# Where the split activations lie in SBUF: x2's high and low parts moved to multiples of 512 bytes

## The chip, the cores and the metric

The kernel runs on one core of one Trainium2 chip. The metric is the device time in microseconds (us), as a median over runs. Inside a core, TensorE (PE) multiplies matrices, VectorE (DVE) and ScalarE (ACT) work on 128-partition tiles, GpSimd (POOL) sums over partitions and issues some transfers, SyncE (SP) issues transfers. SBUF is the memory that the engines read; each tile is a piece of every partition, beginning at a byte address that is the same in all 128 partitions.

## The reference

One block of an RWKV-like network on x of shape (2, 4096, 256), hidden width 1024:

```python
x = x + attn(layernorm(x))     # time mixing, k, v, r, a scan over time, output product
x = x + ffn(layernorm(x))

def ffn(x):                    # x: 256 features
    h = silu(x @ w1.T * w1_s) * (x @ w2.T * w2_s)     # 256 -> 1024, twice
    h = gelu(h @ h1.T * h1_s)                         # 1024 -> 1024
    h = gelu(h @ h2.T * h2_s)                         # 1024 -> 1024
    return h @ w3.T * w3_s                            # 1024 -> 256
```

In attn, k, v, r and the output are products of 256 x 256 weights; the scan carries a log-max and a numerator along 4096 steps.

## The kernel before

Features lie on partitions, time along the free axis. The work is cut into 16 tiles of 512 steps (2 batches x 8). Each tile runs attention and then the FFN. The main loop runs the FFN of tile i and, step by step between its sums, attention of tile i + 1 and the first layernorm of tile i + 2, so that PE always has products to do.

The FFN's weights are ternary, so one fp32r pass holds them exactly. The activations are not, so each activation is split into a high part (rounded to fp32r) and a low part (the rest), and split_product issues two fp32r matmuls for every block of 128 features: L186 with the high part as the moving operand, L187 with the low part, both 128x512, both summed into the same PSUM tile. Attention's products (L179) are plain float32 and show as two matmuls each in the trace.

In the FFN of one tile:

- pa and pb (w1 and w2): 8 columns x 2 sums x 2 blocks x 2 parts = 64 matmuls, moving operands x2_hi and x2_lo. Each of these holds two blocks of 512 float words (2048 bytes) per partition.
- ph (h1, then h2): 2 x 8 columns x 8 blocks x 2 parts = 256 matmuls, moving operands hi and lo, 16 buffers of 2048 bytes each.
- po (w3): 2 x 8 x 2 = 32 matmuls, moving operands hi and lo.

ACT rounds the high parts (L193, L612), DVE takes the low parts (L194, L615). x2 itself is the output of the second layernorm, and x2_hi and x2_lo are made of it by split (L191).

Addresses come from the pools, which are laid one behind another in the order in which they are made: flags, const, x, wide, one, tmp, hid, stream. Within a pool each tag has its buffers, of the size of its largest tile, rounded up to 32 bytes. A tile in an early pool that grows or shrinks therefore moves everything behind it.

The names that the change touches: mean_wr (L136), a 128x128 fp32r tile that holds 1/256, with which the first tile's means are summed on PE (mean_w is the same tile read as float32) and which keep_warm (L372) multiplies with itself to keep PE busy in the first 39 us (results unread); num (L247), the numerator's states; each (L400), in the first tile's layernorm; and any_inexact (L636), which in the last tile's FFN sums a count over the partitions with one small product (everywhere, L641), to decide whether a general form of the block must run afterwards (it does not for these inputs).

Of the kernel before, what the change touches and what calls it, by code (L numbers as in the profile page):

```python
# [9 lines left out]
F32 = mybir.dt.float32  # L10
F32R = mybir.dt.float32r
# [3 lines left out]
P = 128  # L15
B, T, D, HID = 2, 4096, 256, 1024
TS = 512
# [49 lines left out]
def split_block(ctx, tc, flags, x, vecs, w_attn, w1, w2, h1, h2, w3, out):  # L67
# [3 lines left out]
    tensor, vector, scalar = nc.tensor, nc.vector, nc.scalar  # L71

    const = ctx.enter_context(tc.tile_pool(name="const", bufs=1))
    xpool = ctx.enter_context(tc.tile_pool(name="x", bufs=3))
    wide = ctx.enter_context(tc.tile_pool(name="wide", bufs=4))
    one = ctx.enter_context(tc.tile_pool(name="one", bufs=1))
    tmp = ctx.enter_context(tc.tile_pool(name="tmp", bufs=3))
    hid = ctx.enter_context(tc.tile_pool(name="hid", bufs=16))
# [54 lines left out]

    each_mean = hid.tile([P, P], F32, tag="hi", name="each_mean")
    vector.memset(each_mean, 1.0 / D)
    mean_wr = const.tile([P, P], F32R, name="mean_wr")  # L136
    vector.tensor_copy(mean_wr, each_mean)
    mean_w = mean_wr.bitcast(F32)
    vector.memset(eps, LN_EPS)
# [32 lines left out]
    def col(base, j):  # L172
        return vec[:, base + j : base + j + 1]
# [64 lines left out]
    def wkv(h, k, v, r, y, first):  # L238

        w, u = col(DECAY, h), col(FIRST, h)  # L240

        def pair(tag):
            both = one.tile([P, 2, TS], F32, tag=tag, name=tag)
            return [both[:, k, :] for k in range(2)]


        lm, num = (one.tile([P, TS + 1], F32, tag=tag, name=tag) for tag in ("lm", "num"))  # L247
        if first:
            vector.memset(lm[:, 0:1], LOG_ZERO)
            vector.memset(num[:, 0:1], 0.0)  # L250
        else:
            vector.tensor_copy(lm[:, 0:1], log_max[:, h : h + 1])
            vector.tensor_copy(num[:, 0:1], numer[:, h : h + 1])

        sc = pair("sc")


        so = pair("so")  # L260
        with tc.issue_after(marks["y"].ins) if h else nullcontext():
            vector.tensor_tensor_scan(lm[:, 1:], w.to_broadcast([P, TS]), k, lm[:, 0:1], ALU.add, ALU.max)  # L262
        vector.scalar_tensor_tensor(sc[1], lm[:, 0:TS], w, k, ALU.add, ALU.subtract)
        vector.tensor_scalar(sc[0], sc[1], NEG_CLAMP, 0.0, ALU.max, ALU.min)
        vector.tensor_scalar(sc[1], sc[1], 0.0, -NEG_CLAMP, ALU.max, ALU.min)
        scalar.activation(sc[0], sc[0], AF.Exp)
        scalar.activation(sc[1], sc[1], AF.Exp, scale=-1.0)
        vector.scalar_tensor_tensor(so[1], k, u, lm[:, 0:TS], ALU.add, ALU.subtract)
        vector.tensor_scalar(so[1], so[1], NEG_CLAMP, -NEG_CLAMP, ALU.max, ALU.min)
        vector.tensor_copy(log_max[:, h : h + 1], lm[:, TS:])  # L270
        scalar.activation(so[0], so[1], AF.Sigmoid, scale=-1.0)
        scalar.activation(so[1], so[1], AF.Sigmoid)
        scalar.activation(r, r, AF.Sigmoid)
        yield
        vector.tensor_tensor(sc[1], sc[1], v, ALU.mult)
        vector.tensor_tensor_scan(num[:, 1:], sc[0], sc[1], num[:, 0:1], ALU.mult, ALU.add)
        vector.tensor_copy(numer[:, h : h + 1], num[:, TS:])
        yield
        vector.tensor_tensor(so[0], so[0], num[:, 0:TS], ALU.mult)
        vector.tensor_tensor(so[1], so[1], v, ALU.mult)  # L280
        vector.tensor_tensor(so[0], so[0], so[1], ALU.add)
        marks["y"] = vector.tensor_tensor(y[:, h, :], so[0], r, ALU.mult)
        yield
# [23 lines left out]
    def attention(i):  # L307
# [18 lines left out]
        for h in range(ND):  # L326
            kvr = []
            for m, name in enumerate("kvr"):
                ps = ps_attn.tile([P, TS], F32, tag="pa", name="ps_" + name)
                product(  # L330
                    ps, lambda c: wa_sb[:, m, c, h * P : (h + 1) * P], [mixed[m][:, c, :] for c in range(ND)]
                )
                kvr.append(ps)
            yield
            yield from wkv(h, *kvr, y, first)
# [20 lines left out]
    def on(engine, operation, *args, **kwargs):  # L356
        with behind(engine):
            last[engine] = getattr(getattr(nc, engine), operation)(*args, **kwargs)  # L358

    def matmul(*args, **kwargs):  # L360
        on("tensor", "matmul", *args, **kwargs)

    def activation(*args, **kwargs):
        on("scalar", "activation", *args, **kwargs)

    def add(out, a, b, op=ALU.add):
        on("vector", "tensor_tensor", out, a, b, op)
# [12 lines left out]
    def first_layernorm(src, xc, means):  # L380

        sq = wide.tile([P, ND, TS], F32, tag="wide", name="sq")
        for mean, p in zip(means, halves):
            for h in range(ND):
                add(xc[:, h, p], src[:, h, p], mean, ALU.subtract)
            activation(sq[:, :, p], xc[:, :, p], AF.Square)
        varis = []
        for p in halves:  # L390
            add(sq[:, 0, p], sq[:, 0, p], sq[:, 1, p])
            var = ps_ffn.tile([P, TS // 2 // P], F32, tag="pf", name="var")
            for b in range(TS // 2 // P):
                t = slice(p.start + b * P, p.start + (b + 1) * P)
                matmul(var[:, b : b + 1], sq[:, 0, t], mean_w[:, 0:1], start=True, stop=True)
            varis.append(var)
            yield
        spread = []
        for var in varis:
            each = tmp.tile([P, TS // 2 // P], F32, tag="each", name="each")  # L400
            activation(each, var, AF.Sqrt, bias=eps)
            on("vector", "reciprocal", each, each)
            rstd = ps_ffn.tile([P, TS // 2], F32, tag="pf", name="rstd")
            for b in range(TS // 2 // P):
                matmul(
                    rstd[:, b * P : (b + 1) * P], each[:, b : b + 1].to_broadcast([P, P]), ident, start=True, stop=True
                )
            spread.append(rstd)
            yield
        for rstd, p in zip(spread, halves):  # L410
            for h in range(ND):
                add(xc[:, h, p], xc[:, h, p], rstd, ALU.mult)
            yield

    def first_tile(second):
# [3 lines left out]
        lm, num, sc, so = ([] for _ in range(4))  # L419
        for h in range(ND):  # L420
            pool, tags = ((one, ("lm", "num")), (stream, ("h2", "h2")))[h]
            for states, tag, start in zip((lm, num), tags, (LOG_ZERO, 0.0)):
                states.append(pool.tile([P, TS + 1], F32, tag=tag, name="state"))
                vector.memset(states[h][:, 0:1], start)
            for scales, tag in ((sc, "sc"), (so, "so")):
                if h:
                    scales.append([hid.tile([P, TS], F32, tag=t, name="scale") for t in ("hi", "lo")])
                else:
                    both = one.tile([P, 2, TS], F32, tag=tag, name="scale")
                    scales.append([both[:, k, :] for k in range(2)])  # L430
# [5 lines left out]
        for p in halves:  # L436
# [3 lines left out]
            means.append(mean)  # L440
        keep_warm(unread, 11, 2 * P)
        norm = first_layernorm(x_sb, xn, means)


# [120 lines left out]
        x2_hi = one.tile([P, ND, TS], F32R, tag="x2_hi", name="x2_hi")  # L565
        x2_lo = one.tile([P, ND, TS], F32R, tag="x2_lo", name="x2_lo")
        norm = first_layernorm(x_sb, x2, means)
        for _ in range(4):
            next(norm)
# [66 lines left out]
    def any_inexact():  # L636

        total = flags.tile([P, 1], F32, name="total")
        vector.tensor_reduce(total, rounded, mybir.AxisListType.X, ALU.add)
        everywhere = ps_attn.tile([P, 1], F32, tag="pa", name="everywhere")  # L640
        tensor.matmul(everywhere, mean_w, total, start=True, stop=True)  # L641
        inexact = flags.tile([P, 1], mybir.dt.int32, name="inexact")
        vector.tensor_scalar(inexact, everywhere, 0.0, None, ALU.is_gt)
        return inexact
# [4 lines left out]
    normal, got = {}, {}  # L649
    second = normalise(1)  # L650
    first_tile(second)
    with behind("gpsimd"):
        load_rest()
# [307 lines left out]
```

## Time and profile before

| what | value |
|---|---|
| median of 3 runs | 1541.54 us (1541.45 to 1542.15) |
| the profiled execution | 1540.95 us |
| its span, first to last instruction | 1539.4 us |
| mean granted TensorE clock | 0.999 |
| PE busy | 1529.8 us, 6260 matmuls |
| DVE, ACT, POOL busy | 69%, 68%, 16% of the span |
| starts of the FFN of tiles 0, 1, 2, 15 | 39.2, 134.0, 228.2, 1452.0 us |
| distance of two such starts, tiles 1 to 10 | 94.15 us |
| last matmul | 1532.2 us |

A row of the profile names the line, the engine, the operation, and written tile <- read tiles; then the count, busy time and mean duration, and the idle time of the engine before it. Matmuls overlap: the next begins before the one before it has ended. The rate at which PE works is therefore the distance between starts, which the timeline shows, and not the duration.

### The profile page before, as it was taken

To read this page: it belongs to the slowest core of one execution; us is meant where nothing else is said; L and a number is where in the kernel's file an instruction comes from. 1 tells how busy PE (TensorE), PEld (TensorE's weight loads), DVE (VectorE), ACT (ScalarE), POOL (GpSimd) and SP (SyncE) were. 2 spreads that over 40 slices of the span, in tenths; PEclk is the share of its full clock that TensorE was granted. 3 is DMA by queue.
4 is the path that set the end of the run, shared out by engine and by line. 5 is a ranking of instruction groups with operands and counts; after the bars stand their busy time and mean duration, and the time that the engine had idled before them with its cause. 6 is when DMAs were issued, how large, how long until landed. Compare 5 with 4: busy or idle time off the path is not lost.

```text
span 1539.4 us, 16523 instructions
## 1 busy us (share of the span) xinstructions
PE 1529.8 (99%) x6260; PEld 1172.8 (76%) x6260; DVE 1069.8 (69%) x1598; ACT 1047.3 (68%) x1348; POOL 240.5 (16%) x118
## 2 busy tenths in 40 slices
PE   9999999999999999999999999999999999999998
PEld 6778787777877778777787777877777787777886
DVE  7886676866768677785777768677686777855531
ACT  6685957759587595866858668595775858656542
POOL 4131021110211101112011121101111021100100
PEclk9999999999999999999999999999999999999999
DMA  7612030220302103031130311203122030210302
GB/s 274 137 55 89 14 118 33 82 69 14 134 18 96 55 26 133 7 110 42 45 113 14 117 35 59 93 10 120 35 77 74 14 130 21 96 41 28 117 9 83
DMA packets 39702, 109.16 MB, mean 71 GB/s; under 512 B 3712, under 2 KB 12672, under 8 KB 39104
## 3 DMA queue, kind: packets, MB, share of 16 engines
q1 hardware_dynamic: 25760, 79.86, 15.8%
q0 software_dynamic: 13296, 27.53, 5.7%
q8 instruction: 51, 0.84, 0.2%
q10 hardware_dynamic: 560, 0.66, 0.1%
q14 instruction: 35, 0.29, 0.1%
HBM read 99.64 MB, written 12.58 MB: 73 GB/s over the span
## 4 chain that ended last, share of the span: by engine, by line
PE 98%; DVE 1%; ACT 1%; issue 0%; DVEq 0%; ACTq 0%
PE ph L186 30%; PE ph L187 30%; PE pa L186 4%; PE pb L186 4%; PE po L187 4%; PE po L186 4%; PE pa L187 4%; PE pb L187 4%; PE ps_k L179 3%; PE ps_o L179 3%; PE ps_r L179 3%; PE ps_v L179 3%; PE ps_k L358 0%; PE unread L358 0%; DVE scale L358 0%; PE ps_v L358 0%
## 5 line engine op out<-in xcount | busy, mean ns | idle before, releaser
L186 PE MATMUL ph<-hi,h_sb 128*128 128x512 f32 x2048 | 815.7, 399 | 0.2 <-ACT hi L193 0.2
L187 PE MATMUL ph<-lo,h_sb 128*128 128x512 f32 x2048 | 811.5, 397 | 0.0
L186 PEld LDWEIGHTS ph<-hi,h_sb 128*128 128x128 f32 x2048 | 384.6, 188 | 98.5 <-issue 18.2
L187 PEld LDWEIGHTS ph<-lo,h_sb 128*128 128x128 f32 x2048 | 384.5, 188 | 96.9 <-issue 15.3
L207 POOL PARTITION_ALL_REDUCE total<-both x60 | 205.1, 3419 | 857.6 <-DVE both L205 442.7
L615 DVE TENSOR_TENSOR lo<-full,hi 128x512 fp32r<-128x512 f32 x256 | 197.2, 773 | 140.0 <-ACT full L614 137.1
L612 ACT ACTIVATE hi<-ph,vec 128x512 fp32r<-128x512 f32 x256 | 175.6, 686 | 125.7 <-PE ph L187 124.6
L596 ACT ACTIVATE gated<-pa,vec 128x512 f32<-128x512 f32 x128 | 87.4, 683 | 139.0 <-PE pa L187 137.2
L614 ACT ACTIVATE full<-ph,vec 128x512 f32<-128x512 f32 x256 | 175.3, 685 | 0.3
L597 DVE SCALAR_TENSOR_TENSOR gated<-pb,vec,gated 128x512 f32<-128x512 f32 x128 | 95.9, 749 | 70.9 <-PE pb L187 66.6
L612 ACT ACT_TABLE_LOAD x103 | 132.1, 1283 | 1.8
L231 DVE RECIPROCAL rstd<-rstd 128x256 f32<-128x256 f32 x60 | 102.8, 1731 | 2.1 <-ACT rstd L227 2.1
L193 ACT ACTIVATE hi<-gated 128x512 fp32r<-128x512 f32 x128 | 80.4, 628 | 33.8 <-DVE gated L597 33.5
L186 PE MATMUL pa<-x_hi,w_sb 128*128 128x512 f32 x256 | 101.9, 398 | 0.1
L186 PE MATMUL pb<-x_hi,w_sb 128*128 128x512 f32 x256 | 101.8, 398 | 0.0
L187 PE MATMUL pb<-x_lo,w_sb 128*128 128x512 f32 x256 | 100.5, 392 | 0.0
L187 PE MATMUL pa<-x_lo,w_sb 128*128 128x512 f32 x256 | 100.4, 392 | 0.0
L194 DVE TENSOR_TENSOR lo<-gated,hi 128x512 fp32r<-128x512 f32 x128 | 96.3, 760 | 4.8
L187 PE MATMUL po<-lo,w_sb 128*128 128x512 f32 x256 | 99.6, 389 | 0.0
L186 PE MATMUL po<-hi,w_sb 128*128 128x512 f32 x256 | 99.6, 389 | 0.0
L621 DVE SCALAR_TENSOR_TENSOR x_sb<-po,vec,x_sb 128x512 f32<-128x512 f32 x32 | 24.0, 751 | 72.1 <-PE po L187 72.1
L262 DVE TENSOR_TENSOR_SCAN lm<-vec,lm,ps_k 128x512 f32<-128x512 f32 x30 | 38.4, 1279 | 40.7 <-PE ps_k L179 40.7
(145 smaller groups left out, 1741.3 us busy)
## 6 DMA issues: line engine op xcount, KB each, us to landing
h_sb<-h_hbm SPq DMA_DIRECT2D x128, 512.0 KB, 3.2
raw<-in_h SPq DMA_DIRECT2D x32, 256.0 KB, 2.7
x_sb<-in_x POOLq DMA_DIRECT2D x15, 512.0 KB, 4.1
out<-x_sb POOLq DMA_DIRECT2D x15, 512.0 KB, 3.2
h_sb<-in_h POOLq DMA_DIRECT2D x1, 4096.0 KB, 18.7
h_hbm<-in_h POOLq DMA_DIRECT2D x8, 512.0 KB, 8.6
w_sb<-in_w POOLq DMA_DIRECT2D x3, 1024.0 KB, 9.6
raw<-in_w SPq DMA_DIRECT2D x12, 256.0 KB, 2.5
```

Of the source, the lines that this page charges most:

```text
L179: tensor.matmul(psum, weights(c), src[c], start=c == 0, stop=c == n - 1)
L186: tensor.matmul(psum, weights(c), hi, start=c == 0, stop=False)
L187: tensor.matmul(psum, weights(c), lo, start=False, stop=c == n - 1)
L193: marks["rounded"] = scalar.activation(hi, full, AF.Copy)
L194: marks["rest"] = vector.tensor_tensor(lo, full, hi.bitcast(F32), ALU.subtract)
L207: marks["sum"] = nc.gpsimd.partition_all_reduce(everywhere, both, channels=P, reduce_op=ReduceOp.add)
L231: vector.reciprocal(rstd[:, p], rstd[:, p])
L596: scalar.activation(full, pa, AF.Silu, scale=col(S1, f))
L597: vector.scalar_tensor_tensor(full, pb, col(S2, f), full, ALU.mult, ALU.mult)
L612: scalar.activation(hi, ps, AF.Gelu, scale=col(scales, f))
L614: marks["rounded"] = scalar.activation(full, ps, AF.Gelu, scale=col(scales, f))
L615: marks["rest"] = vector.tensor_tensor(lo, full, hi.bitcast(F32), ALU.subtract)
```

## The change

mean_wr takes a buffer of hid's tag "lo" in place of one of its own in const (512 bytes less there). num's buffer, in the pool "one" ahead of sc, so, both, total, x2_hi, x2_lo and xn, is made 32 words longer (2080 to 2208 bytes with rounding). each's three buffers, in tmp, grow from 32 to 160 bytes, so that what lies behind them (the tag "full", then hid and stream) stays where it was: -512 + 128 + 384 = 0. Since the buffer of mean_wr is given to activations later, the product at the end of the last tile reads a tile of ones, set just before, instead.

```diff
-    mean_wr = const.tile([P, P], F32R, name="mean_wr")
+    mean_wr = hid.tile([P, P], F32R, tag="lo", name="mean_wr")
...
-        lm, num = (one.tile([P, TS + 1], F32, tag=tag, name=tag) for tag in ("lm", "num"))
+        lm = one.tile([P, TS + 1], F32, tag="lm", name="lm")
+        num = one.tile([P, TS + 33], F32, tag="num", name="num")[:, : TS + 1]
...
-            each = tmp.tile([P, TS // 2 // P], F32, tag="each", name="each")
+            each = tmp.tile([P, 40], F32, tag="each", name="each")[:, : TS // 2 // P]
...
-                states.append(pool.tile([P, TS + 1], F32, tag=tag, name="state"))
+                states.append(pool.tile([P, TS + (33 if tag == "num" else 1)], F32, tag=tag, name="state")[:, : TS + 1])
...
-        tensor.matmul(everywhere, mean_w, total, start=True, stop=True)
+        ones = tmp.tile([P, P], F32, tag="full", name="ones")
+        vector.memset(ones, 1.0)
+        tensor.matmul(everywhere, ones, total, start=True, stop=True)
```

Where tiles begin in a partition, in bytes, and the remainder by 512:

| tile | before | after |
|---|---|---|
| w1_sb, w2_sb, h1_sb, w3_sb | 25088, 33280, 41472, 74240 (all 0) | the same |
| mean_wr | 82432 (0) | 181760 (0) |
| x_sb, first buffer | 83264 (320) | 82752 (320) |
| wide tiles, first buffer | 95552 (320) | 95040 (320) |
| sc, so | 116096, 120192 (384) | 115712, 119808 (0) |
| x2_hi, x2_lo | 128384, 132480 (384) | 128000, 132096 (0) |
| full, first buffer | 142848 (0) | the same |
| hi, lo, first buffers | 148992, 181760 (0) | the same |

The order of the instructions is the same on every engine, but for the memset of ones on DVE (behind the low part of column 5 in the last tile's second hidden layer) and the product everywhere, which stands five matmuls later on PE, inside column 7's sum, and waits for that memset.

## The prediction

> **What bounds the kernel now.** I read the first part of the page first (busy time per engine), then the chain that ended last, then the costliest groups.
>
> ```profile
> PE 1529.8 (99%) x6260; PEld 1172.8 (76%) x6260; DVE 1069.8 (69%) x1598; ACT 1047.3 (68%) x1348; POOL 240.5 (16%) x118
> ...
> PE 98%; DVE 1%; ACT 1%; issue 0%; DVEq 0%; ACTq 0%
> ...
> L186 PE MATMUL pb<-x_hi,w_sb 128*128 128x512 f32 x256 | 101.8, 398 | 0.0
> L187 PE MATMUL pb<-x_lo,w_sb 128*128 128x512 f32 x256 | 100.5, 392 | 0.0
> ...
> L187 PE MATMUL po<-lo,w_sb 128*128 128x512 f32 x256 | 99.6, 389 | 0.0
> L186 PE MATMUL po<-hi,w_sb 128*128 128x512 f32 x256 | 99.6, 389 | 0.0
> ```
>
> TensorE is never without work: the chain is 98% PE, and the view of waits gives PE 2.6 us of waiting in all, nearly all of it before 37 us. So the end is set by the beat at which one product follows another. The durations in the groups (389 to 398 ns) overlap and are not that beat; the starts in the timeline are. Two windows of PE's timeline, the same form of product (128x512, fp32r) on both sides; columns are start and duration in us:
>
> ```profile
> 418.81 0.40 PE L186 MATMUL pa<-x_hi,w_sb 128*128 128x512 f32 x1
> 419.04 0.39 PE L187 MATMUL pa<-x_lo,w_sb 128*128 128x512 f32 x1
> 419.27 0.40 PE L186 MATMUL pb<-x_hi,w_sb 128*128 128x512 f32 x1
> 419.51 0.39 PE L187 MATMUL pb<-x_lo,w_sb 128*128 128x512 f32 x1
> ...
> 420.91 0.39 PE L187 MATMUL pa<-x_lo,w_sb 128*128 128x512 f32 x1
> ```
>
> ```profile
> 503.83 0.39 PE L186 MATMUL po<-hi,w_sb 128*128 128x512 f32 x1
> 504.06 0.39 PE L187 MATMUL po<-lo,w_sb 128*128 128x512 f32 x1
> ...
> 505.65 0.39 PE L186 MATMUL po<-hi,w_sb 128*128 128x512 f32 x1
> 505.87 0.39 PE L187 MATMUL po<-lo,w_sb 128*128 128x512 f32 x1
> ```
>
> From 418.81 to 420.91 lie nine products that read x2's parts: 2.10 / 9 = 233.3 ns each. From 503.83 to 505.87 lie nine that read hi and lo: 2.04 / 9 = 226.7 ns. With the trace's nanoseconds it is sharper: in each of tiles 1 to 15 the 64 products of pa and pb take 14,925 ns from the first start to the start of ph, that is 233.2 ns, in pairs of 237.5 and 229.3; the 32 of po hold 226.65 to 226.68 in every tile. The granted clock is 1.00 in both stages.
>
> What differs is where the moving operand begins. Counting the pools' sizes, hi, lo, the weights and mean_wr all begin at a multiple of 512 bytes; x2_hi and x2_lo begin at 128384 and 132480, both 384 past one. They are the only moving operands of an fp32r product that do.
>
> **The change part by part.**
>
> *x2's place.* mean_wr leaves the constants (minus 512 bytes for all that follows), num grows from 2080 to 2208 bytes (plus 128), so x2_hi and x2_lo move by 384 down, to 128000 and 132096: remainder 0. The 64 products of a tile should then take the beat of po: 64 x 226.67 = 14,507 ns, 418 ns less. The first three products of ph still carry 15 ns of excess after x2 (beats 231, 233, 231); they go too. That is 433 ns for each of tiles 1 to 15. Tile 0 has 545 ns of excess, of which 107 are its first beat (334 ns, after the products that keep the clock up), which I leave: 438 ns. Sum: 15 x 0.433 + 0.438 = 6.93 us.
>
> Is a beat of 226.7 granted at once? After the two-pass f32 products (ps_r at 438.5 us) the next nine beats of ph, from 440.43 on, run to 232 on average and only then 226.7, about 0.05 us of settling. Ahead of pa lies po, already settled, so I expect none; with it, 16 x 0.05 = 0.8 us would come back. I take 0 and keep 0.8 for the range.
>
> *Does PE then wait for somebody?* The tightest place is the first sum of ph, whose last product reads lo of column 7. In the steady tiles that lo ends 2.84 us after ph's start, and the product that reads it starts at 3.42: 0.57 us of cover. DVE waits 0.32 us for pb ahead of column 7's gating (431.68 us), so it has no backlog and its work moves along with PE; even if all 0.433 us came off the cover, 0.14 would be left. x2 of the next tile is ready 8 to 13 us before its pa. Cost 0; if the cover were gone, at most the 0.43 us of a tile.
>
> *ones and the count.* One memset on DVE and no change on ACT, POOL and SP's order. The nearest row is each_mean's memset of the same size, 165 ns, once. It stands behind lo of column 5 in the last tile's second hidden layer, which ends at 1519.9 us. The product everywhere moves five products later, into column 7's sum, so about 1522.4 us; it now waits for the memset, done 2 us before. Behind it on DVE is queued lo of column 6, started at 1522.83 before; it may slip by some 0.3 us, and po needs it near 1527.9. The product itself cost PE about 0.25 us with its settling (beats 26, 112, 313, 236, 228, 233, 231 around 1521 us) and costs that again; 0 to 0.1 us either way. Cost 0.
>
> *mean_wr among the lo buffers.* It takes the first of 16; the two scales and the two scaled weights of the first tile take others. Its last reader is PE's last unread product (about 39 us), ahead of all FFN products on the same engine, so nobody waits for its buffer. It still begins at a multiple of 512. Cost 0.
>
> *The other tiles that move.* sc, so, both, total and xn go from remainder 384 to 0 (rstd of the second norm from 416 to 32), and only DVE, ACT and POOL touch them. The first tile shows that DVE does not mind: the same sum of shares takes 0.69 us at 24.40 us (h = 0, remainder 384) and 0.69 us at 28.82 us (h = 1, among hi and lo, remainder 0). About ten such instructions lie on the first tile's path; 10 ns each way makes 0.1 us. x_sb and the wide tiles keep their remainder (320). Cost 0, with 0.1 us to both sides.
>
> So 6.93 us come off. The profiled execution took 1540.95 us (span 1539.4); it should become 1534.0 (span 1532.5). The median of the runs is 1541.54, 0.59 above that execution, so the forecast is 1541.54 - 6.93 = 1534.6 us.
>
> *Rules that speak against it.* Other operands in the trace do not mind their place: the two-pass f32 products of ps_k, whose mx begins 320 past a multiple of 512, start every 429 ns (four from 435.05 to 436.76 us), and so do those of the first tile whose xn is shifted by 4 bytes. They stream at about half the rate, so a slow fetch may hide. [...]
>
> **The rivals.**
>
> 1. *Something other than the place sets the 233.3.* pa and pb alone change the bank after every 4 products (ph and po after 16), and read the same four moving blocks over and over. Then nothing changes: 1541.5 us. Against it: in tile 0 pa and pb alternate product by product at first, and the beat is the same 237 and 229; the slow half even falls on x_lo there and on x_hi later, so it goes with the order, not with the tile or the bank. The last tile, with no attention beside it, has the same beat, so it is no other engine. 7%. The same time would result if the place did not move; the sizes above leave no room for that.
>
> 2. *The new place is worse (slower).* All fast operands of the trace, hi, lo and mean_wr, begin at 512 past a multiple of 1024; x2's parts will begin at 0. If the fetch minds the place within 1024, x2 lands in a class that no row shows. Priced as the excess doubled: 1024 products x 6.6 ns = 6.8 us more, 1548.3 us. It decides from a beat over 236.3 ns (3.08 us / 1024 more). Against it: each operand is 2048 bytes long and passes both kinds of boundary anyhow. 4%.
>
> 3. *Better than the rest.* By the same unseen class the beat could fall below 226.7. A two-pass product's pass takes 429.2 ns; if half of that, 214.6, were one pass's floor, up to 1024 x 12.1 = 12.4 us more would go: 1522.2 us. No row supports it. 3%.
>
> 4. *Part of it comes back*, by settling at each start of pa or a lo that comes late: half of the gain, 1538.1 us. The cover of 0.57 us speaks against it. 4%.
>
> **How the numbers follow.** The forecast has 82%. Its own range is 1533.9 to 1536.2: the spread of the three runs (0.7 us) either way, and on the slow side the 0.8 of settling and 0.1 for moved tiles. I stretch the upper end to 1537.0, so as to take in a good part of rival 4, and the lower one to 1533.5 for the 0.1 us bounds and the profiled execution's 0.59 us. A measurement of this kernel tells about 0.2% (3.1 us) from no change, so faster means under 1538.5: 82 + 3 and most of rival 4, 88%. The same: 7% and a little of rival 4, 8%. Slower: 4%.
>
> **What would show it.** In the profile after, starts of pa and pb 226.7 ns apart, hi and lo alike; their group means at 389 as in po; 14.51 us instead of 14.93 from pa's first start to ph; starts of pa 93.72 us apart instead of 94.15; ph, po and the f32 products unchanged. A beat still at 237 and 229 makes rival 1 right; any other beat, rival 2 or 3; a new wait of ph for lo (L194), rival 4.

## The result, and the profile after

The changed kernel takes 1534.89 us (median of 6 runs, 1534.75 to 1535.13) against 1541.58 us before (6 runs): a ratio of 0.9957, 95% interval 0.9947 to 0.9967. The median fell by 6.69 us. The forecast was 1534.6 us (6.93 less), range 1533.5 to 1537.0.

The page of the changed kernel, the lines that answer to those shown of before (busy time per engine, the chain, the groups of pa and pb):

```profile
PE 1523.0 (99%) x6260; PEld 1172.8 (76%) x6260; DVE 1071.1 (70%) x1599; ACT 1047.5 (68%) x1348; POOL 241.9 (16%) x118
...
PE 98%; DVE 1%; ACT 1%; DMA 0%; issue 0%; DVEq 0%
...
L186 PE MATMUL pb<-x_hi,w_sb 128*128 128x512 f32 x256 | 99.6, 389 | 0.0
...
L187 PE MATMUL pb<-x_lo,w_sb 128*128 128x512 f32 x256 | 99.6, 389 | 0.0
```

PE's busy time is 6.8 us shorter with the same 6260 matmuls; DVE and ACT do the same work but for one memset. The means of pa and pb went from 398 and 392 to 389, what po had already. The starts say it directly (PE's timeline in tile 4; columns are start and duration in us):

```profile
419.04 0.39 PE L186 MATMUL pa<-x_hi,w_sb 128*128 128x512 f32 x1
419.27 0.39 PE L187 MATMUL pa<-x_lo,w_sb 128*128 128x512 f32 x1
419.49 0.39 PE L186 MATMUL pa<-x_hi,w_sb 128*128 128x512 f32 x1
...
421.08 0.39 PE L187 MATMUL pa<-x_lo,w_sb 128*128 128x512 f32 x1
```

Nine beats from 419.04 to 421.08: 2.04 / 9 = 226.7 ns, high and low alike. In tiles 1 to 15 the 64 products of pa and pb take 14,506 or 14,507 ns (14,925 before), the first three beats of ph have no excess left, and starts of pa are 93.72 us apart (94.15 before).

The span of the profiled execution fell by 6.1 us, not by 6.93 (that of before was 0.59 us under its median, as the prediction says). Tiles 1 to 15 gave what was forecast: 14 distances between starts, 6.07 us together, and 0.43 in tile 15. Three things of 0.1 to 0.3 us lie outside them. The first start of pa came at 39.47 us instead of 39.16; DVE waited 3.3 instead of 3.0 us for the first x. The kernels below, whose heads are alike but for small memsets, have it between 39.2 and 40.0, so that is no property of the change that these runs could show. Tile 0 gave back most of its part (below). The stretch from the start of the last matmul to the end was 0.12 us longer (7.18 and 7.30; the kernels below have 7.1 to 7.5).

### The profile page after: what moved, and what is told of

Its sections match the earlier page's. It is cut to its first block, busy times and chain, and to the rows that moved or that the text cites. A ratio compares the mean times of both kernels' runs of the same rounds, so it can differ in the third digit from the quotient of the medians.

```text
span 1533.3 us, 16524 instructions
## 1 busy us (share of the span) xinstructions
PE 1523.0 (99%) x6260; PEld 1172.8 (76%) x6260; DVE 1071.1 (70%) x1599; ACT 1047.5 (68%) x1348; POOL 241.9 (16%) x118
## 4 chain that ended last, share of the span: by engine, by line
PE 98%; DVE 1%; ACT 1%; DMA 0%; issue 0%; DVEq 0%
PE ph L186 30%; PE ph L187 30%; PE po L187 4%; PE po L186 4%; PE pa L186 4%; PE pa L187 4%; PE pb L186 4%; PE pb L187 4%; PE ps_k L179 3%; PE ps_o L179 3%; PE ps_v L179 3%; PE ps_r L179 3%; PE ps_k L359 0%; DVE scale L359 0%; DMA x_sb<-in_x 0%; PE ps_v L359 0%
## 5 line engine op out<-in xcount | busy, mean ns | idle before, releaser
L263 DVE TENSOR_TENSOR_SCAN lm<-vec,lm,ps_k 128x512 f32<-128x512 f32 x30 | 38.4, 1278 | 39.2 <-PE ps_k L179 39.2
```

## The experiments

The beats below are times between the first starts of stages, divided by the products between them, so they hold nothing of a matmul's modelled end. Runs 2, 3, 4, 7, 8 and 9 are single executions: their beats carry the argument, not their times.

**1. The change without the new place.**

```diff
-        num = one.tile([P, TS + 33], F32, tag="num", name="num")[:, : TS + 1]
+        num = one.tile([P, TS + 1], F32, tag="num", name="num")
...
-            each = tmp.tile([P, 40], F32, tag="each", name="each")[:, : TS // 2 // P]
+            each = tmp.tile([P, TS // 2 // P], F32, tag="each", name="each")
```

(and the same for num's states in the first tile)

> The change without the paddings of num and each: mean_wr among the lo buffers and the tile of ones stay, x2_hi and x2_lo begin at 127872 and 131968 (remainder 384 again), and hi and lo begin at a multiple of 1024 instead of 512 past one. If x2's place makes the whole gain: 14,925 ns again for the 64 products of pa and pb in tiles 1 to 15, ph, po at 226.7 ns, 1541.5 us. If the other parts of the change (mean_wr's buffer, ones, the order at the end) bring it: 14,507 ns and 1534.9 us. If the place by 1024 mattered for hi and lo: their beat leaves 226.7.

Measured: 1541.45 us, ratio 1.0 (0.9991 to 1.0009). pa and pb take 14,925 ns in tiles 1 to 15, po holds 226.7 ns with hi and lo at multiples of 1024. The groups of pb have the means of before again:

```profile
L186 PE MATMUL pb<-x_hi,w_sb 128*128 128x512 f32 x256 | 101.8, 398 | 0.0
L187 PE MATMUL pb<-x_lo,w_sb 128*128 128x512 f32 x256 | 100.4, 392 | 0.0
```

So mean_wr's buffer, the tile of ones and the later product everywhere cost and bring nothing that can be measured, and the whole gain comes with the two paddings. They move sc, so, both, total and xn besides x2's parts; runs 2 to 4, which move x2's parts alone, tie it to those.

**2. Sixteen places in one kernel.** The paddings of num and each are left out, as in run 1.

```diff
+    PLACES = [(8 * i, 8 * i) for i in range(16)]      # words, high and low part
+    def placed(i):
+        both = one.tile([P, 2 * ND * TS + 128], F32R, tag="x2_hl", name="x2_hl")
+        hi, lo = PLACES[i]
+        return [both[:, at : at + ND * TS].rearrange("p (a b) -> p a b", a=ND) for at in (hi, ND * TS + lo)]
...
-        x2_hi = one.tile([P, ND, TS], F32R, tag="x2_hi", name="x2_hi")
-        x2_lo = one.tile([P, ND, TS], F32R, tag="x2_lo", name="x2_lo")
+        x2_hi, x2_lo = placed(i)
```

> x2_hi and x2_lo lie in one tile with 512 bytes to spare, and tile i of the 16 has both begin 32 x i bytes later: remainders 384, 416, 448, 480, 0, 32, ... 352, one for each of the 16 tiles. If only a multiple of 512 is good (the product then touches one 512-byte piece less): 14,507 ns for pa and pb in tile 4 and about 14,925 in all others. If a smaller step is enough (128 or 256): 14,507 also at remainders 128 or 256 (tiles 8 and 12). If the excess grows with the distance: a ramp over the tiles. Sum over the 15 bad tiles about 1541.1 us in the first case.

Mean beat of the 64 products by the remainder of x2's parts (ns; tile 0 at 384 is left out, since its first beat is long):

| remainder by 512 | 0 | 32 | 64 | 96 | 128 | 160 | 192 | 224 |
|---|---|---|---|---|---|---|---|---|
| beat | 226.7 | 233.4 | 229.2 | 233.5 | 233.2 | 234.2 | 233.3 | 233.4 |
| remainder by 512 | 256 | 288 | 320 | 352 | 384 | 416 | 448 | 480 |
| beat | 226.7 | 233.4 | 229.2 | 233.5 | - | 234.2 | 233.3 | 233.4 |

The whole time is 1540.63 us. The two rows are the same: the step is 256 bytes, not 512. Tile 12 (remainder 256) and tile 8 (128) in PE's timeline:

```profile
1173.92 0.39 PE L187 MATMUL pa<-x_hl,w_sb 128*128 128x512 f32 x1
...
1175.96 0.39 PE L186 MATMUL pa<-x_hl,w_sb 128*128 128x512 f32 x1
```

```profile
797.55 0.40 PE L186 MATMUL pa<-x_hl,w_sb 128*128 128x512 f32 x1
...
799.65 0.39 PE L187 MATMUL pa<-x_hl,w_sb 128*128 128x512 f32 x1
```

Nine beats in 2.04 us there, in 2.10 here. There is no ramp, and 64 is a half-good place: "one more piece of 512 bytes" explains neither. A step of 16 or 32 bytes cannot set it alone either: all 16 places are multiples of 32, and their beats go from 226.7 to 234.2.

**3. Finer places.** The same kernel with the remainders 4, 8, ... in PLACES.

> The same with other remainders, tile by tile: 4, 8, 12, 16, 20, 24, 28, 0, 48, 64, 508, 504, 496, 256, 128, 492. If only a multiple of 512 is good: 14,507 ns in tile 7 alone, 14,925 in the other fourteen (tile 0 apart). If lines of 16 or 32 bytes matter, remainders 16, 48, 64, 496 or 32's multiples differ from 4, 8, 12, 20, 492. If a small offset costs less because the last piece holds few columns: a ramp from 4 up.

| remainder by 512 | 0 | 8 | 12 | 16 | 20 | 24 | 28 | 48 | 64 | 128 |
|---|---|---|---|---|---|---|---|---|---|---|
| beat, ns | 226.7 | 233.5 | 229.0 | 231.6 | 236.0 | 233.3 | 226.7 | 233.3 | 229.2 | 233.2 |
| remainder by 512 | 256 | 492 | 496 | 504 | 508 | | | | | |
| beat, ns | 226.7 | 226.7 | 233.3 | 233.4 | 226.7 | | | | | |

28, 492 and 508 are as good as 0. 20 is the worst of the table; tile 0, at 4, is left out of it for its long first beat, and the other 63 beats there average 236.7. None of the expectations foresaw this; a small offset is neither always bad nor cheap. The whole time is 1539.43 us.

**4. High or low part alone.** PLACES = [(32, 32), (32, 128), (0, 32), (0, 0)] * 4.

> The remainders of (x2_hi, x2_lo) go round over the tiles: (0, 0), (0, 384), (384, 0), (384, 384), four times. If each product pays for its own moving operand: 14,507, 14,716, 14,716, 14,925 ns for pa and pb. If the excess needs both parts off (or is set by the pair's worse half): the two mixed cases equal 14,507 or 14,925. Whole time about 1541.5 - 3.4 = 1538.2 us in the first case.

Measured: 14,507 (tiles 4, 8, 12), 14,721, 14,720 and 14,925 ns; 1538.03 us. The costs of the two parts add up, about 6.6 ns for each product whose moving operand lies off. Tile 5, low part off:

```profile
513.09 0.39 PE L186 MATMUL pb<-x_hl,w_sb 128*128 128x512 f32 x1
513.32 0.40 PE L187 MATMUL pb<-x_hl,w_sb 128*128 128x512 f32 x1
513.55 0.39 PE L186 MATMUL pa<-x_hl,w_sb 128*128 128x512 f32 x1
...
514.47 0.39 PE L186 MATMUL pb<-x_hl,w_sb 128*128 128x512 f32 x1
```

Six beats in 1.38 us, 230 ns; in the trace's nanoseconds they alternate, 226 and 234.

**5. The weights moved instead.** Up to here the place could be a matter of the moving operand alone. A rival appeared: PE loads the next product's weights (LDWEIGHTS, 188 ns) while a product runs, and every weight tile lay at a multiple of 512. Two rows of the changed kernel, a product and the load beside it (PEld):

```profile
419.49 0.39 PE L186 MATMUL pa<-x_hi,w_sb 128*128 128x512 f32 x1
419.50 0.19 PEld L187 LDWEIGHTS pa<-x_lo,w_sb 128*128 128x128 f32 x1
```

```diff
     hid = ctx.enter_context(tc.tile_pool(name="hid", bufs=16))
+    gap = ctx.enter_context(tc.tile_pool(name="gap", bufs=1))
...
+    nc.gpsimd.memset(gap.tile([P, 96], F32, name="unused"), 0.0)
```

> The changed kernel with 384 unused bytes ahead of the streamed blocks of h2: the stationary operand of the 2048 products of the second hidden layer begins at remainder 384 by 512 (128 by 256), its moving operands hi and lo stay at 0. If only the moving operand's own place counts: all beats 226.7 ns and 1534.9 us. If what counts is the moving operand's place against that of the weights that PE loads at the same time: 233.2 ns in the second hidden layer alone, 2048 x 6.5 ns = 13.4 us more, 1548.3 us.

Measured: 1546.10 us, ratio 1.003 (1.0018 to 1.0042). pa and pb stay at 226.7; the second hidden layer, whose moving operands did not move, goes to 232.4 ns (233.7 in tiles 0, 10 and 14). Tile 4, second hidden layer:

```profile
489.83 0.39 PE L189 MATMUL ph<-lo,h_sb 128*128 128x512 f32 x1
...
491.92 0.39 PE L188 MATMUL ph<-hi,h_sb 128*128 128x512 f32 x1
```

Nine beats in 2.09 us. In the time: 1.003 - 0.9957 = 0.0073 of 1541.5 us is 11.3 us, and 2048 x 5.7 ns makes 11.7. The place of the moving operand alone does not set the beat.

**6. Both moved.**

```diff
-            each = tmp.tile([P, 40], F32, tag="each", name="each")[:, : TS // 2 // P]
+            each = tmp.tile([P, TS // 2 // P], F32, tag="each", name="each")
```

> The changed kernel without the padding of each: hi, lo and the streamed blocks of h2 all begin at remainder 128, x2's parts and the resident weights w1, w2, h1, w3 stay at 0. If the moving operand's own place counts: 233.2 ns in both hidden layers and in po, 4608 x 6.5 ns = 30.1 us more, 1565.0 us. If the place against the weights counts: 233.2 in the first hidden layer and po, but 226.7 in the second hidden layer, where both have moved alike: 2560 x 6.5 = 16.7 us more, 1551.6 us.

Measured: 1549.15 us, ratio 1.0049 (1.0031 to 1.0067), 14.3 us over the changed kernel. The first hidden layer and po run at about 232.4 and 232.6 ns, the second hidden layer, once a sum has settled, at 226.7. PE's timeline of tile 4, first in the second hidden layer (hi, lo and the weights at 128), then in po (hi and lo at 128, w3 at 0):

```profile
489.71 0.39 PE L186 MATMUL ph<-hi,h_sb 128*128 128x512 f32 x1
489.94 0.39 PE L187 MATMUL ph<-lo,h_sb 128*128 128x512 f32 x1
...
491.75 0.39 PE L187 MATMUL ph<-lo,h_sb 128*128 128x512 f32 x1
```

```profile
507.66 0.40 PE L187 MATMUL po<-lo,w_sb 128*128 128x512 f32 x1
507.90 0.40 PE L186 MATMUL po<-hi,w_sb 128*128 128x512 f32 x1
...
509.76 0.39 PE L186 MATMUL po<-hi,w_sb 128*128 128x512 f32 x1
```

Nine beats in 2.04 us against nine in 2.10. Moved alike, the two are as fast as at 0; moved apart, they are slow. For places 128 apart by 256 it is the moving operand's place against the weights' that counts. The two places do not act independently: moving one operand's tile changes the beat by 5.7 ns (226.7 to 232.4, run 5), and moving the other along takes it back (226.7). Whether the weights in use count, or the next ones that are loaded meanwhile, these runs do not tell: in each stage both have the same remainder.

**7. Forty-eight places of the weights.**

```diff
-                    block = stream.tile([P, NH, P], F32R, tag="h2", name="h2_sb")
+                    at = list(range(16))[i]
+                    block = stream.tile([P, NH * P + 40], F32R, tag="h2", name="h2_sb")
+                    block = block[:, at : at + NH * P].rearrange("p (a b) -> p a b", a=NH)
```

> The changed kernel with every streamed block of h2 made 160 bytes longer and begun 4 x i bytes late in tile i. The three buffers begin at 0, 160 and 64 by 256, so the stationary operands of the second hidden layer lie at 48 different places by 256 (0 to 31 and 40 to 55 words), hi and lo at 0. If the place against the weights counts, weights at word w give the beat that x2 gave at word -w: 226.7 for words 0, 1, 5 (x2 at -4 and -20 bytes), 233.3 for 16 and 48 (x2 at 192), 229.2 for 48 if the sign is the other. If the weights' place does not count: 226.7 at every one. A beat below 226.7 anywhere would show that 226.7 is not the floor.

Run 2 as the comparison, in 32-byte steps (weights at +w against x2 at -w, by 256; the beat of a column's sum, its first four beats left out):

| weights at, bytes | 32 | 64 | 96 | 160 | 192 |
|---|---|---|---|---|---|
| beat, ns | 233.5 | 233.5 | 233.9 | 233.5 | 229.2 |
| x2 at | 224 | 192 | 160 | 96 | 64 |
| beat, ns | 233.4 | 233.3 | 234.2 | 233.5 | 229.2 |

They agree within 0.3 ns, with 229.2 at the sign that the difference of places asks for. (The expectation has that sign wrong for word 48: by its own rule x2 at -192, which is 64 by 256, is the counterpart, with 229.2.) In steps of 4 bytes they do not agree: weights at 20 bytes give 233.2 where x2 at 492 (-20) gave 226.7, and weights at 16 bytes give 226.7 where x2 at 496 (-16) gave 233.3. So the difference orders the places that are multiples of 32 bytes apart, and inside 32 bytes it does not.

Nor do the places alone set the beat. Columns 2 and 5 of tile 13 read the same moving tiles and the same buffer of weights (116 by 256); the first and the last start of each:

```profile
1331.63 0.39 PE L186 MATMUL ph<-hi,h_sb 128*128 128x512 f32 x1
...
1335.08 0.40 PE L187 MATMUL ph<-lo,h_sb 128*128 128x512 f32 x1
```

```profile
1342.81 0.40 PE L186 MATMUL ph<-hi,h_sb 128*128 128x512 f32 x1
...
1346.31 0.39 PE L187 MATMUL ph<-lo,h_sb 128*128 128x512 f32 x1
```

Fifteen beats in 3.45 us (230.0 ns, alternating 229 and 231) against fifteen in 3.50 (233.3, repeating 236, 235, 229): the same addresses hold two steady patterns. Run 5 has two as well, 232.4 and, in tiles 0, 10 and 14, 233.7. Something besides the places must therefore count too (these runs do not show what), and a difference of 1 to 3 ns between two places need not come from the places. No column's mean beat lay below 226.6 in any of these places. The whole time is 1544.93 us.

**8 and 9. Fewer columns of weights.** If the two reads meet, as the author supposed, a shorter load should meet less. (The loads of 128, 96, 64 and 32 columns take 188, 161, 134 and 109 ns in run 8's trace. Such a product also writes fewer partitions of its result, which these runs do not separate from the load.)

```diff
-            tensor.matmul(psum, weights(c), hi, start=c == 0, stop=False)
+            m = cols if 0 < c < n - 1 else P        # cols: (128, 64, 32, 96)[i % 4] in the second hidden layer
+            tensor.matmul(psum[:m], weights(c)[:, :m], hi, start=c == 0, stop=False)
```

(the same for the low part; run 9 has run 5's gap besides)

> The changed kernel, in which products 3 to 14 of the 16 of every sum of the second hidden layer (feature blocks 1 to 6) load and use only the first 128, 64, 32 or 96 columns of the stationary operand, by the tile's number modulo 4; the rest of their outputs is left out. All places stay at multiples of 512. If the 12.1 ns that a beat of 226.7 has over half of an f32 pass (214.6) come from the weights that PE loads beside the moving operand: 226.7, 220.6, 217.6, 223.7 ns. If they are a fixed cost of a product, or hang on the moving operand alone: 226.7 in all four.

> The same with 384 unused bytes ahead of the streamed blocks, so that hi and lo lie at 0 and these weights at 128 by 256 (beat 232.4 with all columns). If the excess is a meeting of the two reads: 232.4, 223.5, 219.1, 227.9 ns for 128, 64, 32, 96 columns. If the moving operand alone pays once the weights lie off: 232.4 in all four.

Measured in run 8, from the start of a sum's third product to that of its last: 226.7, 229.8, 232.1 and 230.2 to 230.8 ns for 128, 64, 32 and 96 columns, 1540.27 us. The same stage of tile 6 (32 columns):

```profile
679.81 0.40 PE L187 MATMUL ph<-hi,h_sb 128*32 128x512 f32 x1
...
681.67 0.40 PE L187 MATMUL ph<-hi,h_sb 128*32 128x512 f32 x1
```

Eight beats in 1.86 us, 232 ns (the rows left out hold the four products around a sum's end, which keep all columns): with a quarter of the columns the products were slower. Run 9: 232.4 (233.7 in tile 0), 229.8, 230.5 to 231.5 and 228.2 to 231.4 ns, 1543.30 us. Both readings fail: with fewer columns the beat rose in run 8 and fell in run 9, in neither in the order of the load's length, and it is not fixed. What stays is that the beat also depends on how many columns are loaded and used. Why it does, and why one place held two patterns in run 7, no run shows; this is left open.

**10. Everything at a multiple of 256.**

```diff
-    prev = const.tile([P, 32], F32, name="prev")[:, 0:ND].unsqueeze(2)
+    prev = const.tile([P, 80], F32, name="prev")[:, 0:ND].unsqueeze(2)
```

(and 49 in place of 33 in num)

> The changed kernel with prev 48 words longer and num 16 words longer: x_sb and the wide tiles (mx, move, y, the moving operands of attention's f32 products) go from 64 to 0 by 256, x2, full, hi, lo and the streamed weights from 0 to 256 by 512. If 256 is the step: 226.7 ns everywhere as in the changed kernel. If the settling after f32 products (beats of 224 to 236 for about nine products; 0.2 us in a tile's 93.72) is a leftover of their own bad place, it goes: 93.52 us between starts of pa, 3.0 us less, 1531.9 us. If it comes with every change from f32 to fp32r: 93.72 and 1534.9 us. If 512 is the step after all: every product of the FFN at another beat than 226.7 (1541 us and more).

Measured: 1534.80 us, ratio 0.9958 (0.9944 to 0.9971). x2, hi, lo and h2's blocks lie 256 past a multiple of 512 here, w1, w2, h1 and w3 at a multiple of 512, and everything runs as in the changed kernel; starts of pa are 93.72 us apart (tiles 1 to 10), to the nanosecond. So 256 is the step for hi and lo too, and the 0.2 us of settling per tile after the f32 products do not come from where attention's operands lie. No run was faster than the changed kernel by more than the scatter of its runs.

## Why the prediction was right

**The beat and its price: right.** 433 ns per tile was forecast, 433 to 434 measured. 226.7 was granted at once, without the settling that the range kept 0.8 us for, and the three beats of ph after x2 lost their excess. Only tile 0, which has no po ahead of it, settled (0.07 us).

**The reason given: wrong in two points.** The prediction called x2's place by 512 bytes what differs. The step is 256 (runs 2 and 10), and, between places 32 or more bytes apart, it is not the moving operand's own place but its place against the weights (runs 5 to 7: 226.7 ns moved alike, 232.4 with the weights alone at 128). The forecast survived because the trace of before held the weights of all stages at multiples of 512, so that "x2 on a multiple of 512" and "x2 in line with the weights" were the same edit. That is luck in the reason, not in the price: the beat to be had was read from po, but the rule by 512 would have failed for an edit that moves the weights.

**PE's waits: right in the steady tiles, missed in tile 0.** In the steady tiles, lo of column 7 ended 2.95 us after ph's start, and the product that reads it started at 3.40: 0.12 us had come off the cover, within the 0.43 that the prediction allowed for, and 0.45 were left. But tile 0 has its own order and no cover: PE waited there for ACT's high part of column 7 already before. PE's waits before and after:

```profile
PE ph L186 <- ACT hi L193: 0.2, 1, 0.2
```

```profile
PE ph L186 <- ACT hi L193: 0.5, 1, 0.5
```

The beat there went from 609 to 884 ns. In run 1, with x2 slow, the view of waits has 0.2 again, in run 4 (tile 0 at the good place) 0.5: counted from the tile's first product, PE gets there 0.36 us earlier, and ACT's high part only 0.11 (it ends 18.46 instead of 18.57 us after that product's start). Of tile 0's 0.44 us, 0.27 went so, and another 0.07 in its first beats; 0.07 was left. The step that failed is the cost of 0 for all tiles, taken from the steady ones. The 0.107 us that the forecast leaves to tile 0's first beat are measured (334 ns before, 341 after). That the unread products ahead of it keep the clock up is shown by no run: every kernel here has them, and the granted clock is 1.00 in each stretch from 0 to 54 us, before and after.

**ones, the count and mean_wr: right.** The memset took 165 ns at 1513.6 us, the product everywhere cost the beats 26, 112, 313, 236, 228, 233, 230, as before (26, 112, 313, 236, 228, 233, 231); run 1 has all of it and no change of time.

**The rivals.** The first (something else sets the beat) falls with run 1, but its heart was half right: the weights, which it did not name, count. The second and third (a class by 1024) fall with run 1 and the changed kernel: hi and lo at multiples of 1024, and x2 there, all run at 226.7. The fourth (part comes back) is what tile 0 shows, but with 0.36 us and not half of the gain. The beat below 226.7 that the third has came at no place tried: no mean beat in the tables above is lower, and no column of run 7 has a mean below 226.6.

## What to carry to other kernels

Where PE is never idle, read the distance between starts and compare stages with the same form of product: 3% in one stage (233.2 ns against 226.7) was visible before any edit. Lay moving operands and weights of fp32r products at the same remainder by 256 bytes (0 and 128 were tried: 226.7 ns with both alike, 232.4 to 233.2 with one of them 128 off), and look at both when a pool ahead of them changes by a few bytes. When two explanations call for the same edit, the number will not tell them apart; move the other operand.

## What was not expected of the hardware

- Moving only the weights by 128 bytes (by 256) slows products whose moving operand stays, 226.7 to 232.4 ns (run 5); moving both alike does not (226.7, run 6).
- Inside 32 bytes there is no simple order: x2 at 28, 492 and 508 is as good as 0 (226.7 ns), at 20 (236.0) and 4 (236.7) it is worse than at any other place of x2 tried.
- The same addresses held two steady patterns, 230.0 and 233.3 ns, in two columns of one tile.
- Products with 32 or 64 columns of weights had a longer beat (232.1 and 229.8 ns) than those with 128 (226.7), with weights and moving operands at multiples of 512.
